# A layer norm's inverse deviation on GpSimd, a split group of attention matmuls, and fewer gather buffers in a two-layer metaformer kernel

## The chip, the cores and the metric

The kernel runs on one core of one Trainium2 chip. The metric is device time in microseconds (us) of one execution; the time given for a kernel is the median of its runs. The core has five engines that run their own instruction streams in order and meet at semaphores: PE (TensorE, matmuls), DVE (VectorE), ACT (ScalarE), POOL (GpSimd) and SP (SyncE, which here only issues DMAs). PEld is PE's weight load.

## What is computed

Input `x` is 8 images of 128 channels and 32 by 32 pixels, float32. Two layers follow each other; every one has a mixing step and a feed-forward step, each behind a normalisation and with a residual:

```python
x = x + attention(_ln_c(x))          # 8 heads, keys and queries over all 1024 pixels, softmax per row of 32 keys
t = t + stu(_ln_t(t))                # 16 spectral filters (causal convolutions) mixed by matrices, 4 resolutions
x = x + deformable_conv(_ln_c(x))    # 3 taps, each sample from 4 neighbouring pixels of a computed place
t = t + experts(_ln_t(t))            # 8 experts, the best 2 of a router
```

with

```python
def _ln_c(v, eps=1e-6):
    m = jnp.mean(v, axis=1, keepdims=True)
    s = jnp.var(v, axis=1, keepdims=True)
    return (v - m) / jnp.sqrt(s + eps)
```

In the attention `softmax` runs over the 32 keys of one image row (`axis=-1` of scores shaped batch, head, h, w, x, y), so that one query has 32 separate softmaxes, whose weighted values are added. The change touches the two normalisations that run inside the attention stage, the order of the attention's value matmuls, and the loads of the deformable convolution's samples.

## The kernel before

**Stages.** After a short start (about 30 us) comes the attention of all eight images, up to about 995 us. Then the spectral stage runs to about 2911 us: PE works through 4 groups of two images with 16 filters each (`filter_image`, L1355, and `mix`, L1343), and beside it, in slices that `advance` hands out, the second layer of the images of the group before (`DeformAndExperts.image`). The second layer of the last two images (`alone` is true) stands by itself at the end.

**The attention** (`attention_bounded`, L492 to L743) is written as a list of steps. `at(round, order, step)` puts a step into a round; the list is sorted by round, then by order, then by the place in the code, and emitted in that order under a manual schedule, so each engine's instruction order is what this list says. An image has 8 units (4 quarters of 256 queries times 2 groups of 4 heads), a unit has 4 rounds, so an image has 32 rounds and the stage 256. With `t0` the first round of a unit and `r` from 0 to 3:

- round `t0 + r`, order 0, `scores`: 8 matmuls on PE into `s`, a PSUM tile of which there is one (`bufs=1`); then one exponential on ACT, L606, 128 x 2048, into `e`, of which there are 11. The next round's scores overwrite `s`, so they wait for this exponential.
- round `t0 + r`, order 1, `add_tiles`: POOL adds the two halves of `e` into `t` (L615).
- round `t0 + 5`, order 4, `sums`: 16 matmuls into `z`; order 5, `reciprocals` on DVE (L629).
- round `t0 + 6`, order 2.5, `spread_out`: 4 matmuls that spread the reciprocals into `rb`.
- round `t0 + 6 + r`, order 3, `divide`: DVE multiplies `e` by `rb` (L643, 128 x 2048).
- round `t0 + 8 + r`, order 2, `values`: 8 matmuls of `e` into `av` (L653).

Order 6 is for the projections of the next image (`project_at`), the stores of results (`results`, one per two units, in round `t0 + 12` of the second) and the layer norm of the next image. I call the four rounds of a unit phases 0 to 3 (the round number modulo 4). Since units follow every four rounds, a phase 0 round holds scores, the first value group and a projection or a result's matmuls; phase 1 holds scores, the second value group and the 16 sums; phase 2 scores, the third group and the spreading; phase 3 scores, the fourth group and often a projection.

**The layer norm pieces** (`layer_norm_pieces`, L65) are 21 steps: 8 of statistics on DVE, then `guess` (4 instructions), three times `newton` (4 each) and `offset` (1), all on tiles of 128 x 8, and 8 of `norm` on ACT (L104), which need `offset`'s result `lp_nm`. `norm_at` gives their rounds, order 6: for images 2 to 7, counted from the first round of the image before, statistics in rounds 3 to 10, guess in 10, newton in 11, 11 and 12, offset in 12, and the eight `norm` in rounds 13 and 14, four in each. `FirstGroup.pieces` (L1187) uses the same steps for the first two images of the spectral stage, in the last image's rounds (order 7): the first image's statistics begin in round 8, its norms in round 20; the second's steps come 10 rounds later.

**The gathers** (`image`, L1030 to L1062): 24 points (8 token tiles, 3 taps), each an indirect DMA that POOL issues (L1043), 128 rows of 2 KB, into a buffer `g` of which there are 9; then 4 multiply-adds on DVE (L1058) per point. `fetch` is called 6 times ahead of the loop (3 times if `alone`), each followed by a `yield` unless `alone`, and once per point in it. `yield` hands control back to `advance`, so it moves where later steps stand in the instruction streams.

Of the kernel before, what the change touches and what calls it, by code (L numbers as in the profile page):

```python
# [11 lines left out]
F32 = mybir.dt.float32  # L12
I32 = mybir.dt.int32
AF = mybir.ActivationFunctionType
ALU = mybir.AluOpType
# [3 lines left out]
P = 128  # L19
B = 8  # L20
C = 128
T = 1024
NT = T // P
# [41 lines left out]
def layer_norm_pieces(nc, pool, src, dst, eps):  # L65

    t = {}

    def stats(i):
        if i == 0:
            for name, shape in (
                ("st", [P, NT, 6]), ("mv", [P, NT, 2]), ("v", [P, NT]), ("y", [P, NT]),
                ("w", [P, NT]), ("nm", [P, NT]),
            ):
                t[name] = pool.tile(shape, F32, tag=f"lp_{name}", name=f"lp_{name}")
            t["b"] = pool.tile([P, NT], I32, tag="lp_b", name="lp_b")
        nc.vector.bn_stats(t["st"][:, i, :], src()[:, i, :])
        nc.vector.bn_aggr(t["mv"][:, i, :], t["st"][:, i, :])  # L80

    def guess():
        v, y = t["v"], t["y"]
        nc.vector.tensor_scalar(v, t["mv"][:, :, 1], eps, None, ALU.add)
        nc.vector.tensor_scalar(t["b"], v.bitcast(I32), 1, None, ALU.logical_shift_right)
        nc.vector.tensor_scalar(
            y.bitcast(I32), t["b"], -1, 0x5F3759DF, ALU.mult, ALU.add
        )
        nc.vector.tensor_scalar(v, v, -0.5, None, ALU.mult)

    def newton():
        v, y, w = t["v"], t["y"], t["w"]
        nc.vector.tensor_mul(w, y, y)
        nc.vector.tensor_mul(w, w, v)
        nc.vector.tensor_scalar(w, w, 1.5, None, ALU.add)
        nc.vector.tensor_mul(y, y, w)

    def offset():
        nc.vector.scalar_tensor_tensor(
            t["nm"], t["mv"][:, :, 0], -1.0, t["y"], ALU.mult, ALU.mult  # L100
        )

    def norm(i):
        nc.scalar.activation(  # L104
            dst()[:, i, :], src()[:, i, :], AF.Identity, bias=t["nm"][:, i : i + 1],
            scale=t["y"][:, i : i + 1],
        )

    return (
        [partial(stats, i) for i in range(NT)] + [guess, newton, newton, newton, offset]  # L110
        + [partial(norm, i) for i in range(NT)]
    )
# [379 lines left out]
def attention_bounded(ctx, tc, ident, x, x1d, given, begin_group):  # L492
# [8 lines left out]
    nc = tc.nc  # L501
# [8 lines left out]
    sb = ctx.enter_context(tc.tile_pool(name="a_sb", bufs=2))  # L510
# [8 lines left out]
    for i in range(2):  # L519
        v = cp.tile([P, NT, VB], F32, name=f"vt{i}")  # L520
# [123 lines left out]
            e, e, un["rb"].unsqueeze(2).to_broadcast([P, NH, 2, QU]), ALU.mult  # L644
        )

    def values(img, un, r, qrt):
        hg = un["at"][1]
        if hg == 0 and r == 0:
            qrt["av"] = rp.tile([P, 512], F32, tag="av", name="av")  # L650
        for c in range(2):
            for j in range(NH):
                nc.tensor.matmul(  # L653
                    qrt["av"][32 * j : 32 * j + 32, 0:QU],
                    img["v"][:, 2 * r + c, P * hg + 32 * j : P * hg + 32 * j + 32],
                    un["e", r][:, j, c, :],
                    start=(hg == 0 and r == 0 and c == 0),
                    stop=(hg == HG - 1 and r == 3 and c == 1), skip_group_check=True,
                )
# [24 lines left out]
    def at(round_no, order, do, *args):  # L684
        work.append((round_no, order, len(work), do, args))

    def spread_rounds(pieces, rounds):
        for piece, round_no in zip(pieces, rounds):
            at(round_no, 6, piece)

    for b in range(B):
        img = {}
        first = 4 * UNITS * b
        project = [
            (keys, img, 0, 0), (keys, img, 0, 1), (queries, img, 0, 0),
            (keys, img, 1, 0), (keys, img, 1, 1), (queries, img, 1, 0),
            (key_values, b, img, 0), (key_values, b, img, 1),
            (queries, img, 0, 1), (queries, img, 1, 1),
        ]
        if b == 0:  # L700
            turn = {"tokens": (0, 0)}
            project_at = (-1, -1, -1, 1, 2, 3, 7, 8, 11, 12)
        else:
            project_at = [first + n for n in (-12, -9, -5, -4, -1, 3, 4, 7, 11, 12)]
            if b == 1:
                turn = {"load": 0, "tokens": (4, 6)}
                norm_at = (5,) * 4 + (7,) * 4 + (8, 8, 9, 9, 9) + (10,) * 4 + (11,) * 4
            else:
                turn = {"load": first - 36, "tokens": (first - 30, first - 26)}
                norm_at = [first - n for n in (  # L710
                    29, 28, 27, 26, 25, 24, 23, 22, 22, 21, 21, 20, 20, 19, 19, 19, 19, 18, 18, 18, 18
                )]
            turn["channels"] = (first - 17, first - 13)
        if b:
            at(turn["load"], 6, load, b)
            spread_rounds(
                layer_norm_pieces(nc, sb, lambda i=img: i["xt"], lambda: given.ht, 1e-6), norm_at
            )
            for par in range(2):
                at(turn["channels"][par], 5.5, channels, par)  # L720
        for par in range(2):
            at(turn["tokens"][par], 5.5, tokens, img, par)
        for step, when in zip(project, project_at):
            at(when, 6, *step)
        for qc in range(QC):
            qrt = {}
            for hg in range(HG):
                un = {"at": (qc, hg)}
                t0 = first + 4 * (HG * qc + hg)
                for r in range(4):  # L730
                    at(t0 + r, 0, scores, img, un, r)
                    at(t0 + r, 1, add_tiles, un, r)
                    at(t0 + 5, 4, sums, un, r)
                    at(t0 + 6 + r, 3, divide, un, r)
                    at(t0 + 8 + r, 2, values, img, un, r, qrt)
                at(t0 + 5, 5, reciprocals, un)
                at(t0 + 6, 2.5, spread_out, un)
            at(t0 + 11, 5, take, qrt)
            at(t0 + 12, 6, results, b, img, qc, qrt)
# [48 lines left out]
class DeformAndExperts:  # L788
# [182 lines left out]
    def image(self, b, x2, alone):  # L971
        nc, sb = self.nc, self.sb
# [46 lines left out]
        for tap in range(TAPS):  # L1019
            at = TAPS * C + 9 * tap  # L1020
# [9 lines left out]
        got = []  # L1030
        yield from self.corners(om, got)
        idx, w = got
# [6 lines left out]
        def fetch():  # L1039
            if len(fetched) < len(points):  # L1040
                i, tap = points[len(fetched)]
                g = sb.tile([P, 4 * C], F32, tag="g", name="g", bufs=9)
                nc.gpsimd.indirect_dma_start(  # L1043
                    out=g, out_offset=None, in_=rows,
                    in_offset=bass.IndirectOffsetOnAxis(ap=idx[:, i, tap : tap + 1], axis=0),
                )
                fetched.append(g)

        for _ in range(3 if alone else 6):
            fetch()  # L1050
            if not alone:
                yield
        yield
        yield
        for n, (i, tap) in enumerate(points):
            fetch()
            for k in range(4):
                nc.vector.scalar_tensor_tensor(  # L1058
                    x3[:, i, :], fetched[n][:, k * C : (k + 1) * C], w[:, i, tap, k : k + 1],
                    (tok if tap + k == 0 else x3)[:, i, :], ALU.mult, ALU.add,  # L1060
                )
            yield 1.7  # L1062
# [6 lines left out]
        got = []  # L1069
# [97 lines left out]
class FirstGroup:  # L1167
# [19 lines left out]
    def pieces(self, pool):  # L1187

        got = [(14, self.read), (3, partial(self.load, 0)), (4, partial(self.load, 1))]
        for n in range(2):  # L1190
            pieces = layer_norm_pieces(
                self.nc, pool, lambda n=n: self.ur[n], lambda n=n: self.ur[n], 1e-5
            )
            rounds = [*range(8, 21), *(20 + i // 2 for i in range(8))]
            got += [(r + 10 * n, piece) for r, piece in zip(rounds, pieces)]
        return got


# [258 lines left out]
def metaformer_kernel(  # L1457
# [25 lines left out]
    with tc.If(bounded > P - 1) as branch:  # L1483
        with ExitStack() as part:
            attention_bounded(part, tc, ident, x, x1d, given, begin.pieces)
# [66 lines left out]
```

## Time and profile before

| | us |
|---|---|
| runs of the kernel before | 3128.75, 3130.27, 3132.58 (median 3130.27) |
| the profiled execution's own time | 3137.39 |
| its span, from first to last instruction | 3135.6 |
| PE busy | 2793.4 (89%) |
| DVE, ACT, POOL busy | 1464.0 (47%), 978.7 (31%), 957.2 (31%) |

The durations below come from the profiled execution, 7 us above the median. "Busy" is the time in which an engine has an instruction in work, and the shares are averages over stages with different limits. A line of the timeline gives start, duration, engine, line, operation, output and inputs, count, and in brackets how long the engine had been idle and what ended that. A line of the groups gives the busy time of all, the mean of one in ns, and the idle time ahead of them.

### The profile page before, as it was taken

What the parts mean: (1) busy time and instruction counts of PE and PEld (TensorE: products, weight loads), DVE (VectorE), ACT (ScalarE), POOL (GpSimd) and SP (SyncE); (2) the same over time, 40 slices, a digit from 0 to 9 for tenths busy, and PEclk for the clock granted to TensorE, in tenths of its full rate; (3) what the DMA queues carried; (4) which work ended last, traced back from release to release, by engine and by line L of the source; (5) the groups of instructions that cost most, each with busy time, mean ns of one, the idle gap of its engine ahead of it and who ended that gap; (6) DMA issues with size and microseconds to landing.
All of it is one profiled execution on the core that took longest, in us unless ns stands there. A gap on an engine that the chain in (4) does not pass through costs nothing.

```text
span 3135.6 us, 45294 instructions
## 1 busy us (share of the span) xinstructions
PE 2793.4 (89%) x18896; PEld 1713.5 (55%) x18896; DVE 1464.0 (47%) x3035; ACT 978.7 (31%) x1198; POOL 957.2 (31%) x800
## 2 busy tenths in 40 slices
PE   7989889989986999999899899899899989899506
PEld 3545445545443666666566566566566656566202
DVE  4788788788786200000522440333522143332487
ACT  4666666666653111112112112212112211111100
POOL 4767667667663200000301300300300030300230
PEclk9999999999998999999999999999899999999758
DMA  0000000000001422210614411511611341610540
GB/s 25 2 15 15 1 15 15 2 15 9 2 28 40 115 61 65 76 48 27 201 41 124 124 34 41 171 58 58 184 34 48 107 121 34 191 51 14 175 146 14
DMA packets 177011, 199.80 MB, mean 64 GB/s; under 512 B 17236, under 2 KB 135188, under 8 KB 176800
## 3 DMA queue, kind: packets, MB, share of 16 engines
q1 hardware_dynamic: 147328, 134.97, 14.4%
q0 software_dynamic: 16800, 55.59, 5.8%
q10 hardware_dynamic: 12672, 6.29, 0.7%
q8 instruction: 150, 2.46, 0.3%
q14 instruction: 61, 0.50, 0.1%
HBM read 128.88 MB, written 67.92 MB: 63 GB/s over the span
## 4 chain that ended last, share of the span: by engine, by line
PE 54%; DVE 4%; another core or an unknown queue 3%; issue 1%; DMA 1%; ACT 1%; POOL 0%; ACTq 0%; POOLq 0%; DVEq 0%
PE pu L1355 33%; PE po L1343 15%; PE p_e L1076 3%; DVE x L1058 2%; PE p_g L1002 1%; DVE x L1082 1%; DMA tab<-gs 1%; PE p_out L1093 0%; PE p_out L1096 0%; PE p_turn L905 0%; PE p_l L1120 0%; DMA g<-tab,cn_idx 0%; ACT us L1359 0%; PE p_ut L1299 0%
## 5 line engine op out<-in xcount | busy, mean ns | idle before, releaser
L1359 ACT COPY us<-pu 128x512 f32<-128x512 f32 x512 | 300.1, 586 | 1382.0 <-PE pu L1355 1228.9
L615 POOL TENSOR_TENSOR t<-e 128x1024 f32<-128x1024 f32 x256 | 620.1, 2424 | 312.2 <-ACT e L606 312.2
L1355 PE MATMUL pu<-teto,ur 128*128 128x512 f32 (+3 forms) x2048 | 603.1, 438 | 51.3 <-ACT us L1359 40.1
L643 DVE TENSOR_TENSOR e<-e,rb 128x2048 f32<-128x2048 f32 x256 | 572.7, 2277 | 87.9 <-PE rb L636 85.6
L606 ACT ACTIVATE e<-s 128x2048 f32<-128x2048 f32 x256 | 480.9, 1878 | 293.2 <-PE s L601 291.6
L1355 PEld LDWEIGHTS pu<-teto,ur 128*128 128x128 f32 x2048 | 390.2, 192 | 330.7 <-issue 201.5
L1343 PE MATMUL po<-us,mf 128*128 128x128 f32 (+2 forms) x2048 | 530.8, 383 | 0.0
L601 PE MATMUL s<-q,k 32*128 32x256 f32 x4096 | 303.0, 411 | 37.0 <-ACT e L606 30.1
L1355 PE MATMUL pu<-teto,ht 128*128 128x512 f32 x992 | 292.2, 438 | 23.0 <-ACT us L1359 23.0
L653 PE MATMUL av<-e,vt 128*32 128x256 f32 x4096 | 283.2, 395 | 28.7 <-DVE e L643 23.8
L1043 POOL DMA_INDIRECT g<-tab,cn_idx x192 | 185.0, 964 | 377.2 <-DMA tab<-gs 194.3
L1355 PE MATMUL pu<-teto,xc 128*128 128x512 f32 x992 | 290.1, 435 | 2.9 <-issue 2.9
L1058 DVE SCALAR_TENSOR_TENSOR x<-g,w,x 128x128 f32<-128x128 f32 x704 | 250.3, 357 | 60.0 <-DVE x L1058 24.1
L601 PEld LDWEIGHTS s<-q,k 32*128 32x128 f32 x4096 | 190.2, 189 | 157.8 <-ACT e L606 101.2
L1355 PEld LDWEIGHTS pu<-teto,xc 128*128 128x128 f32 x992 | 188.7, 191 | 157.0 <-issue 116.9
L1343 PEld LDWEIGHTS po<-us,mf 128*128 128x128 f32 x2048 | 272.1, 193 | 4.1 <-issue 3.9
L757 POOL TENSOR_SCALAR rs_v<-rs_v 128x8 f32<-128x8 f32 x18 | 4.4, 246 | 875.2 <-DVE rs_b L755 875.2
L1082 DVE SCALAR_TENSOR_TENSOR x<-p_e,gates,x 128x128 f32<-128x128 f32 x512 | 177.6, 350 | 187.0 <-PE p_e L1076 170.8
L1355 PEld LDWEIGHTS pu<-teto,ht 128*128 128x128 f32 x992 | 189.6, 192 | 135.7 <-issue 67.0
L653 PEld LDWEIGHTS av<-e,vt 128*32 128x32 f32 x4096 | 108.9, 111 | 164.3 <-issue 72.7
L629 DVE RECIPROCAL r<-z 128x256 f32<-128x256 f32 x64 | 112.4, 1757 | 110.8 <-PE z L622 77.4
L1076 PE MATMUL p_e<-ew,tc 128*128 128x512 f32 x256 | 134.8, 633 | 14.0 <-DVE x L1082 8.9
(235 smaller groups left out, 1809.6 us busy)
## 6 DMA issues: line engine op xcount, KB each, us to landing
tab<-gs SPq DMA_DIRECT2D x168, 256.0 KB
mf<-mfd SPq DMA_DIRECT2D x48, 512.0 KB
teto<-in_phi_o SPq DMA_DIRECT2D x63, 256.5 KB
teto<-in_phi_e SPq DMA_DIRECT2D x63, 256.0 KB
mfd<-mf SPq DMA_DIRECT2D x16, 512.0 KB
tab<-gs ACTq DMA_DIRECT2D x24, 256.0 KB
xc<-in_x SPq DMA_DIRECT2D x8, 512.0 KB
x1d<-xt SPq DMA_DIRECT2D x8, 512.0 KB
```

The costliest lines, as they stand in the source:

```text
L601: nc.tensor.matmul(s[:, j, c, :], img["k"][rows, hg, 2 * r + c, :], q[rows, qc * QU : (qc + 1) * QU], start=True, stop=True,)
L606: nc.scalar.activation(e.rearrange("p j c q -> p (j c q)"), s.rearrange("p j c q -> p (j c q)"), AF.Exp, scale=float(HD) ** -0.5,)
L615: nc.gpsimd.tensor_add(t, e[:, :, 0, :], e[:, :, 1, :])
L643: nc.vector.tensor_tensor(e, e, un["rb"].unsqueeze(2).to_broadcast([P, NH, 2, QU]), ALU.mult)
L653: nc.tensor.matmul(qrt["av"][32 * j : 32 * j + 32, 0:QU], img["v"][:, 2 * r + c, P * hg + 32 * j : P * hg + 32 * j + 32], un["e", r][:, j, ...
L1043: nc.gpsimd.indirect_dma_start(out=g, out_offset=None, in_=rows, in_offset=bass.IndirectOffsetOnAxis(ap=idx[:, i, tap : tap + 1], axis=0),)
L1058: nc.vector.scalar_tensor_tensor(x3[:, i, :], fetched[n][:, k * C : (k + 1) * C], w[:, i, tap, k : k + 1], (tok if tap + k == 0 else x3)[: ...
L1076: nc.tensor.matmul(pe, tc[:, i * P : (i + 1) * P], self.ew[:, grp * 4 : grp * 4 + 4, :].rearrange("d e c -> d (e c)"), start=True, stop=True,)
L1082: nc.vector.scalar_tensor_tensor(x3[:, i, :], pe[:, k * C : (k + 1) * C], gate[:, i, grp * 4 + k : grp * 4 + k + 1], x3[:, i, :], ALU.mult ...
L1343: self.nc.tensor.matmul(out, lhsT, rhs, start=bank not in group["opened"], stop=last, skip_group_check=True)
L1355: nc.tensor.matmul(pu[:, i * P : HT], group["ur"][n][:, src * 4 + i, :], flt[:, 0 : HT - i * P], start=(i == 0), stop=(i == 3),)
L1359: nc.scalar.copy(us[:, n, :], pu)
```

## The change

The steps `guess`, `newton` and `offset` are issued on POOL in place of DVE. `guess` has three instructions in place of four (the shift by one bit and the product with -1 become one product with -0.5), `offset` two in place of one, so it is 17 instructions as before. Their rounds change for images 2 to 7: the statistics are in rounds 3, 3, 4, 4, 7, 7, 8, 8, guess in 8, newton in 9, 10 and 10, offset in 10, and the norms in rounds 11 to 14, two in each. For image 1 `norm_at` stays as it is. For the second image of the first group the steps come 4 rounds after the first image's in place of 10.

The second value group of each unit is split: the half for `c = 0` moves to the end of phase 0 (order 6.5), the half for `c = 1` stays in phase 1.

The gathers have 8 buffers in place of 9, and 3 calls of `fetch` stand ahead of the loop for all images, so images that are not `alone` have 3 calls and 3 `yield` fewer there.

```diff
@@ layer_norm_pieces
-            t["b"] = pool.tile([P, NT], I32, tag="lp_b", name="lp_b")
     def guess():
         v, y = t["v"], t["y"]
-        nc.vector.tensor_scalar(v, t["mv"][:, :, 1], eps, None, ALU.add)
-        nc.vector.tensor_scalar(t["b"], v.bitcast(I32), 1, None, ALU.logical_shift_right)
-        nc.vector.tensor_scalar(
-            y.bitcast(I32), t["b"], -1, 0x5F3759DF, ALU.mult, ALU.add
-        )
-        nc.vector.tensor_scalar(v, v, -0.5, None, ALU.mult)
+        nc.gpsimd.tensor_scalar(v, t["mv"][:, :, 1], eps, None, ALU.add)
+        nc.gpsimd.tensor_scalar(
+            y.bitcast(I32), v.bitcast(I32), -0.5, 0x5F3759DF, ALU.mult, ALU.add
+        )
+        nc.gpsimd.tensor_scalar(v, v, -0.5, None, ALU.mult)
 
     def newton():
         v, y, w = t["v"], t["y"], t["w"]
-        nc.vector.tensor_mul(w, y, y)
-        nc.vector.tensor_mul(w, w, v)
-        nc.vector.tensor_scalar(w, w, 1.5, None, ALU.add)
-        nc.vector.tensor_mul(y, y, w)
+        nc.gpsimd.tensor_mul(w, y, y)
+        nc.gpsimd.tensor_mul(w, w, v)
+        nc.gpsimd.tensor_scalar(w, w, 1.5, None, ALU.add)
+        nc.gpsimd.tensor_mul(y, y, w)
 
     def offset():
-        nc.vector.scalar_tensor_tensor(
-            t["nm"], t["mv"][:, :, 0], -1.0, t["y"], ALU.mult, ALU.mult
-        )
+        nc.gpsimd.tensor_mul(t["nm"], t["mv"][:, :, 0], t["y"])
+        nc.gpsimd.tensor_scalar(t["nm"], t["nm"], -1.0, None, ALU.mult)
@@ attention_bounded
-    def values(img, un, r, qrt):
+    def values(img, un, r, cs, qrt):
...
-        for c in range(2):
+        for c in cs:
...
                 norm_at = [first - n for n in (
-                    29, 28, 27, 26, 25, 24, 23, 22, 22, 21, 21, 20, 20, 19, 19, 19, 19, 18, 18, 18, 18
+                    29, 29, 28, 28, 25, 25, 24, 24, 24, 23, 22, 22, 22, 21, 21, 20, 20, 19, 19, 18, 18
                 )]
...
-                    at(t0 + 8 + r, 2, values, img, un, r, qrt)
+                at(t0 + 8, 2, values, img, un, 0, (0, 1), qrt)
+                at(t0 + 8, 6.5, values, img, un, 1, (0,), qrt)
+                at(t0 + 9, 2, values, img, un, 1, (1,), qrt)
+                at(t0 + 10, 2, values, img, un, 2, (0, 1), qrt)
+                at(t0 + 11, 2, values, img, un, 3, (0, 1), qrt)
@@ DeformAndExperts.image
-                g = sb.tile([P, 4 * C], F32, tag="g", name="g", bufs=9)
+                g = sb.tile([P, 4 * C], F32, tag="g", name="g", bufs=8)
...
-        for _ in range(3 if alone else 6):
+        for _ in range(3):
             fetch()
             if not alone:
                 yield
@@ FirstGroup.pieces
-            got += [(r + 10 * n, piece) for r, piece in zip(rounds, pieces)]
+            got += [(r + 4 * n, piece) for r, piece in zip(rounds, pieces)]
```

## The prediction

> **What bounds the kernel now.** I read the busy times by stretch first, to see which engine sets each stage, then one unit of the attention and one layer norm in the timeline, then the waits of PE in the spectral stage.
>
> ```profile
> core 0: us, PE busy (x) PEld busy (x) DVE busy (x) ACT busy (x) POOL busy (x), PEclk, DMA share, GB/s
> 50.00:300.00 250.00, 231.10 (x3012) 128.80 (x3000) 202.50 (x164) 156.42 (x132) 169.83 (x71) 0.97 0.02 8
> ...
> 1400.00:1700.00 300.00, 288.36 (x1174) 187.31 (x1173) 82.24 (x286) 61.88 (x111) 36.11 (x66) 0.98 0.28 83
> ...
> 2900.00:3136.00 236.00, 98.80 (x306) 50.04 (x304) 159.06 (x568) 20.74 (x42) 51.16 (x52) 0.69 0.37 111
> ```
>
> PE is fullest in the attention and the spectral stage, DVE at the end. In the attention no engine is full; a cycle of two engines sets the pace. PE's timeline of an ordinary phase 1, to the next scores:
>
> ```profile
> 502.25 1.15 PE L601 MATMUL s<-q,k 32*128 32x256 f32 x16 [0.39 <-ACT e L606]
> 503.32 1.07 PE L653 MATMUL av<-e,vt 128*32 128x256 f32 x16
> 504.21 1.91 PE L622 MATMUL z<-t,group 128*32 128x256 f32 x32
> 506.05 1.15 PE L601 MATMUL s<-q,k 32*128 32x256 f32 x16
> ```
>
> Scores, then the exponential (L606, 1.88), then the next scores: 1.15 + 1.88 and the hand-overs give 3.17 us, the shortest distance of two exponentials in the trace. A round takes longer where PE has more than 3.17 us of work: in phase 1 it is 1.07 (scores to values) + 1.0 (values) + 1.73 (sums) = 3.80. Over all 256 exponentials of ACT's timeline, images 1 to 6 take 115.5 to 118.2 us each; 32 rounds of 3.17 are 101.4. Of the 16 us between, 8 x 0.63 = 5 belong to phase 1, 1.9 to turning tokens, and about 9 to one place, the layer norm:
>
> ```profile
> 544.33 2.44 POOL L615 TENSOR_TENSOR t<-e 128x1024 f32<-128x1024 f32 x1 [0.45 <-ACT e L606]
> 544.34 2.45 DVE L96 TENSOR_TENSOR lp_y<-lp_y,lp_w 128x8 f32<-128x8 f32 x1
> ...
> 545.48 1.88 ACT L606 ACTIVATE e<-s 128x2048 f32<-128x2048 f32 x1 [0.58 <-PE s L601]
> ...
> 550.83 1.65 ACT L104 ACTIVATE ht<-xt,lp_nm,lp_y 128x128 f32<-128x128 f32 x4 [3.48 <-DVE lp_nm L99]
> ...
> 552.39 1.85 ACT L606 ACTIVATE e<-s 128x2048 f32<-128x2048 f32 x1
> ...
> 554.66 2.08 PE L636 MATMUL rb<-r,spread 64*128 64x256 f32 x8 [3.73 <-DVE r L629]
> ```
>
> Four norms stand ahead of an exponential on ACT and wait for DVE, which is late: a multiply of 8 columns took 2.45 us, just as long as POOL's addition beside it. The exponentials of rounds 13, 14, 15 then lie 6.9 and 6.6 apart here, and 9.6 and 6.5 in the other images. And PE, after 3.73 us without work, runs at half speed: these 8 matmuls take 2.08 us where an ordinary unit's take 1.14. Summed over images 1 to 6 the excess of rounds 13 to 15 over an ordinary round is 53.5 us (8.9 each); image 0 has 7.2 (rounds 10 and 11), the last image 13.4 (rounds 18 to 22 and 30).
>
> In the spectral stage PE is 96% busy, and its idle time has one name:
>
> ```profile
> PE pu L1355 <- ACT us L1359: 63.1, 5, 14.9
> ```
>
> The first such wait of ACT, in its timeline, has no releaser that the profile knows:
>
> ```profile
> 1541.15 0.59 ACT L1359 COPY us<-pu 128x512 f32<-128x512 f32 x1 [16.51 <-remote]
> ```
>
> In each of the six gather phases there, PE stands still for 10.6 to 14.9 us (74 us in all): some 10 us after the gathers' data begin to flow, ACT's copy starts 14 us after the matmul that it waits for, and goes on some 4 us after POOL first paused (at 1536.9, waiting for L1058). Until then POOL issued a gather every 1.25 us.
>
> **What the Trainium skill says.** SBUF — State Buffer, "SBUF: two separate sides": DVE and GpSimd share a port pair as an exclusive lock; a DVE operation with two SBUF inputs or in a two-port mode waits out the GpSimd operation. The trace agrees (2.45 us beside 2.44), and also that a DVE operation with one PSUM input isn't concerned: `divide` takes 2.28 us, and POOL's addition 2.43 beside it against 2.35 for the same size (L1033) in the spectral stage. TensorE: Matmul & The Clock Gate, "What's actually happening": a window of some 3.4 us of idleness halves the clock. Here gaps of 2.8 to 4.9 us were followed by half speed, for about 5.8 us; gaps of 1.5 us weren't.
>
> **The change, part by part.**
>
> *Values.* Half a group is 0.5 us. Phase 1 becomes 1.07 + 0.5 + 1.73 = 3.30. Phase 0 gains 0.5: in odd units it holds a projection (1.07 + 1.0 + 1.1 = 3.17, PE already full) and becomes 3.67, so the pair stays at 6.97; in even units it holds a result's matmuls (0.7), becomes 3.28, and the pair falls from 6.97 to 6.58. The half group needs `divide` of r = 1, which ends some 1.5 us into phase 0, so it doesn't wait. 4 pairs x 8 images + 2 (the last image has no projections late) = 34 x 0.39 = **-13**.
>
> *Norm on POOL.* DVE loses 17 small instructions per norm: 65 us over nine norms by the groups of lines L84 to L99. DVE isn't what bounds a unit; what counts is when `lp_nm` comes. POOL's small instructions in the spectral stage start 0.28 to 0.32 us apart (L757 to L762), so guess takes 0.9, newton 1.17, offset 0.6. For images 2 to 7, with round 9's scores as zero and rounds of 3.30, 3.17, 3.22: POOL does addition 8 to 2.5, then the addition of the results (L678, 2.35), which stands there too, to 4.8, guess to 5.7, addition 9 to 8.1, newton to 9.3, addition 10 to 11.7, two newtons and offset to 14.65. Round 12's scores start at 9.67, its exponential is due at 10.9. On ACT two norms stand ahead of it: they end at 15.45, so it ends at 17.35. PE has 3.67 of work in that round and then idles 4.0 us, so its clock falls: round 13 takes 6.1 in place of 3.3. Excess 4.06 + 2.8 = 6.9, against 8.9: 6 x 2.0 = **-12**. Later norms, two a round, take 0.8 us of ACT's 1.2 between exponentials. The sums of round 13 need addition 11, which ends as round 13 begins. The statistics, two in a round, fill DVE to within 0.2 us; I put that at nothing.
>
> Image 1's norm has no results' addition in its way, but 7 and 10 small instructions in two rounds: `lp_nm` 3.4 us into round 11, four norms, 3.9 + 2.7 = 6.6 against 7.2: **-0.5**. First group: newtons in three successive rounds make POOL late by 1.3 us; rounds 20 and 24 each wait 3.3 to 3.8 and then run at half speed: 12.8 against 13.4, **-0.6**; the norms leave the attention's tail, where the last sums came 2.4 us after the addition that they needed: **-2.4**.
>
> *Gathers.* In the built program POOL's 24 gathers of an image follow each other with nothing between, before and after. The number begun ahead only moves later steps; POOL's distance is set by the buffers. The three slots fewer cost nothing: PE needs the result 25 us after DVE has it (L905 after L780). With 8 buffers POOL waits for the use of the point 8 back: the first pause comes one gather, 1.3 us, earlier in each of the phases that I followed. If PE's stall ends that much earlier: 6 x 1.3 = **-8**. Bounds: -74, if all stalls go; +8, if the pauses only starve DVE. At the end, where DVE is the bound, a buffer less may cost up to 3.
>
> Sum: -13 - 12 - 0.5 - 0.6 - 2.4 - 8 = -36.5; 3137.4 becomes 3100.9, the median 3130.3 becomes **3094**.
>
> **The rivals.**
> - *The gather stalls mostly go.* They end after POOL pauses; earlier pauses might stop them from forming. Against: the start at 1.25 us a gather is the same, and the stall begins before any pause. Half of 74 in place of 8 gives 3065, all 3028.
> - *The norm moves nothing*, because POOL's chain is 2 us later than I reckon, and the gathers give nothing: only the values' 13 and the tail remain, 3115. For it: POOL is two thirds busy there, and each newton round already exceeds a 3.17 round.
> - *Slower: POOL's small instructions wait out `divide`.* If the lock worked that way, each of 14 instructions behind addition 9 could wait up to 2.28 us; all nine norms hold an exponential. At a mean wait of 0.55 us, 7.7 us per norm, +69 - 36: 3163. It decides from 4 us a norm, 0.29 us per instruction. Against: `divide` has a PSUM input, and POOL's addition lost only 0.08 us beside it.
> - That the gather edit doesn't do what it says, since POOL runs eight ahead, is part of my forecast.
>
> **How the numbers follow.** Forecast 0.62 (3076 to 3110 by itself); fewer stalls 0.16; norm moves nothing 0.13; slower 0.09. The range 3056 to 3119 leaves out the slower case and the larger half of the stalls' case, and takes in POOL 2 us late or early per norm. A measurement of this kernel tells 0.2% (6 us) from no change. Faster 0.88, same 0.04, slower 0.08.
>
> **What would show it.** Exponentials in phase 1 3.3 apart outside the norms; ACT waiting for POOL's `lp_nm` some 4.4 us ahead of each of nine first norms (40 in all, against 50.2 for DVE's now); half-speed matmuls in round 13; the six stalls still there, a little shorter; gathers still 1.25 us apart at first. Wrong, if small POOL instructions in the attention take over 0.5 us, or if PE's gaps at L1355 change by more than 20 us.

## The result, and the profile after

The changed kernel took 3094.94 us (median of 4 runs, 3088.86 to 3098.41), the kernel before 3131.43 in the same measurement (3128.75 to 3137.65): a ratio of 0.9879, with a 95% interval of 0.9857 to 0.9900. That is 36.5 us faster. The profiled execution of the changed kernel took 3088.86, its span is 3087.1; it is the fastest of its four, and the profiled one of before (3137.39) lies near the slowest of its own (3137.65), so the two spans lie 48.5 us apart, 12 more than the medians.

A stretch of the attention, in the columns of the prediction's first view:

```profile
50.00:300.00 250.00, 238.44 (x3100) 129.69 (x3092) 198.26 (x138) 160.02 (x135) 181.06 (x123) 0.99 0.04 12
```

In the attention PE gains (231.1 to 238.4 of 250 us), DVE sheds its small operations to POOL, and the granted clock is higher (0.97 to 0.99). PE's first spectral matmul moved from 996.6 to 957.5: **39.1 us, all that the medians show and more, come from the attention.** In the traces of two runs below that have the attention of before, PE's first spectral matmul stands at 991.8 and 995.1, so this difference is good to some 5 us.

I took the distances of successive exponentials in ACT's timeline; that of round 11 is the distance from its exponential to the next. The mean over images 1 to 6 (the images in whose rounds the norms of images 2 to 7 lie), in us, with three of the experiments below beside it (their rounds outside the table agree with those of the changed kernel to 0.02):

| round | before | after | late norms | POOL at the old rounds | DVE at the new rounds |
|---|---|---|---|---|---|
| even unit, phase 0 / 1 | 3.18 / 3.81 | 3.30 / 3.38 | 3.30 / 3.38 | 3.30 / 3.38 | 3.30 / 3.38 |
| odd unit, phase 0 / 1 | 3.18 / 3.81 | 3.71 / 3.37 | 3.71 / 3.37 | 3.71 / 3.37 | 3.71 / 3.37 |
| 10 | 3.17 | 3.16 | 3.16 | 3.16 | 12.94 |
| 11 | 3.17 | 7.17 | 3.17 | 3.17 | 4.10 |
| 12 | 3.19 | 4.10 | 3.71 | 3.71 | 3.58 |
| 13 | 9.16 | 4.15 | 3.74 | 5.84 | 3.39 |
| 14 | 6.51 | 3.20 | 3.24 | 3.35 | 3.26 |
| 15 | 3.39 | 3.17 | 3.17 | 3.56 | 3.17 |
| sum of 32 | 117.5 | 113.0 | 108.2 | 110.8 | 118.4 |

One norm in the changed kernel, in the timeline of POOL, DVE, ACT and PE (rounds 10 to 12 of an image; start, duration, then as before):

```profile
401.23 2.37 POOL L675 TENSOR_TENSOR xt<-xt,at 128x1024 f32<-128x1024 f32 x1
...
405.62 8.88 DVE L640 TENSOR_TENSOR e<-e,rb 128x2048 f32<-128x2048 f32 x4 [1.38 <-PE rb L633]
...
407.85 2.37 POOL L612 TENSOR_TENSOR t<-e 128x1024 f32<-128x1024 f32 x1
...
412.80 0.24 POOL L98 TENSOR_SCALAR lp_nm<-lp_nm 128x8 f32<-128x8 f32 x1
413.01 2.35 POOL L612 TENSOR_TENSOR t<-e 128x1024 f32<-128x1024 f32 x1
413.08 0.88 ACT L101 ACTIVATE ht<-xt,lp_nm,lp_y 128x128 f32<-128x128 f32 x2 [3.79 <-POOL lp_nm L98]
413.86 1.86 ACT L603 ACTIVATE e<-s 128x2048 f32<-128x2048 f32 x1
...
415.77 2.09 PE L598 MATMUL s<-q,k 32*128 32x256 f32 x16 [3.34 <-ACT e L603]
```

The chain is the one that the prediction drew: POOL adds the results (L675) and works off the additions late, `lp_nm` comes at 413.04, two norms and then the exponential follow on ACT, and PE's scores wait 3.34 us for that.

After this gap PE runs at half speed. The views by stretch show for how long (the third figure from the end is the granted clock, 1.00 for full speed). The first three lines are from a norm of the kernel before, behind the gap of 3.73 us in the prediction's lines, the others from the norm just shown:

```profile
554.05:557.46 3.41, 2.80 (x16) 1.90 (x20) 0.78 (x2) 1.73 (x5) 2.38 (x1) 0.50 0.00 0
557.46:560.88 3.42, 3.42 (x32) 1.43 (x27) 3.42 (x2) 1.92 (x2) 0.00 (x0) 0.50 0.03 7
560.88:564.29 3.41, 3.18 (x40) 1.89 (x38) 3.41 (x3) 2.52 (x3) 2.42 (x1) 1.00 0.00 0
...
411.98:415.39 3.41, 0.45 (x8) 0.00 (x0) 2.52 (x2) 2.31 (x3) 3.13 (x5) 1.00 0.00 0
415.39:418.80 3.41, 3.03 (x28) 1.77 (x32) 0.00 (x0) 2.42 (x5) 2.35 (x1) 0.50 0.00 0
418.80:422.20 3.40, 3.40 (x64) 1.88 (x60) 1.42 (x1) 2.15 (x4) 2.29 (x1) 1.00 0.00 0
```

At the norms of images 1 to 6 the half-speed stretches of the kernel before are 6.83 or 10.24 us long (51.2 us together), those of the changed kernel 3.41 us, one of them 6.83 (23.9 us together). The prediction read some 5.8 us for the kernel before from the lengths of the matmuls.

POOL's small operations take what they take in the spectral stage (203 and 235 ns there, L760 and L761 of the kernel before; 203 and 235 here, L92 and L93). In the groups of the changed kernel (busy time, mean ns of one, idle time ahead):

```profile
L93 POOL TENSOR_SCALAR lp_w<-lp_w 128x8 f32<-128x8 f32 x27 | 6.3, 235 | 2.4
```

None of them waits out `divide` (L640), which runs beside them, and the rival that made the kernel slower falls.

The waits of the changed kernel (engine, what waits, for what: us in total, times, longest):

```profile
PE pu L1356 <- ACT us L1360: 40.2, 4, 12.0
PE pu L1356 <- issue: 23.2, 6, 8.5
PE p_gt L1153 <- DVE gates L1149: 20.6, 7, 13.5
...
ACT ht L101 <- POOL lp_nm L98: 28.3, 8, 3.8
ACT xc L101 <- POOL lp_nm L98: 3.2, 1, 3.2
```

ACT waits 31.5 us in nine places for `lp_nm`. PE's six stalls at `pu` are there and shorter, 57 us by their gaps against 74. And one line is new: PE waits 7 times for DVE's `gates`, where the same view of the kernel before has 4 (17.1 us). The last two readings looked like a gain and a trifle; in the experiments the second is part of a loss, and the first couldn't be tried.

### The profile page after: what moved, and what is told of

It is laid out like the page before. It is cut to its first block, busy times and chain, and to the rows that moved or that the text cites. A ratio compares the mean times of both kernels' runs of the same rounds, so it can differ in the third digit from the quotient of the medians.

```text
span 3087.1 us, 45244 instructions
## 1 busy us (share of the span) xinstructions
PE 2792.3 (90%) x18896; PEld 1704.3 (55%) x18896; DVE 1401.7 (45%) x2882; ACT 977.1 (32%) x1198; POOL 976.0 (32%) x953
## 4 chain that ended last, share of the span: by engine, by line
PE 55%; DVE 5%; issue 2%; another core or an unknown queue 2%; DMA 1%; ACT 1%; POOL 0%; ACTq 0%; POOLq 0%; DVEq 0%
PE pu L1356 34%; PE po L1344 15%; PE p_e L1077 3%; DVE x L1059 2%; PE p_g L1003 1%; DVE x L1083 1%; DMA tab<-gs 1%; PE p_out L1094 1%; PE p_out L1097 1%; PE p_turn L906 0%; PE p_l L1121 0%; ACT us L1360 0%; PE p_ut L1300 0%; DMA g<-tab,cn_idx 0%
## 5 line engine op out<-in xcount | busy, mean ns | idle before, releaser
L612 POOL TENSOR_TENSOR t<-e 128x1024 f32<-128x1024 f32 x256 | 607.5, 2373 | 245.0 <-ACT e L603 245.0
L1356 PE MATMUL pu<-teto,ur 128*128 128x512 f32 (+3 forms) x2048 | 604.7, 439 | 40.4 <-ACT us L1360 29.1
L640 DVE TENSOR_TENSOR e<-e,rb 128x2048 f32<-128x2048 f32 x256 | 570.3, 2279 | 95.1 <-PE rb L633 93.7
L650 PE MATMUL av<-e,vt 128*32 128x256 f32 x4096 | 292.6, 393 | 6.1 <-DVE e L640 4.9
L650 PEld LDWEIGHTS av<-e,vt 128*32 128x32 f32 x4096 | 101.7, 110 | 150.3 <-issue 91.1
```

The source lines that it names most:

```text
L612: nc.gpsimd.tensor_add(t, e[:, :, 0, :], e[:, :, 1, :])
L640: nc.vector.tensor_tensor(e, e, un["rb"].unsqueeze(2).to_broadcast([P, NH, 2, QU]), ALU.mult)
L650: nc.tensor.matmul(qrt["av"][32 * j : 32 * j + 32, 0:QU], img["v"][:, 2 * r + c, P * hg + 32 * j : P * hg + 32 * j + 32], un["e", r][:, j, ...
L1356: nc.tensor.matmul(pu[:, i * P : HT], group["ur"][n][:, src * 4 + i, :], flt[:, 0 : HT - i * P], start=(i == 0), stop=(i == 3),)
```

## Experiments

These runs came from three chips (the results name them 1, 13 and 15; the chip of the first measurement isn't on record). There the kernel before takes 3038 to 3039 us in place of 3131, and PE has no stalls in the gather phases, as a wait of the kernel with 8 buffers and 6 ahead shows below. The attention's code is that of before in the kernel with 8 buffers, and the mean of images 1 to 6 is 117.5 us there as in the first profile, so what concerns the attention carries over; what the gathers' edit does to the stalls couldn't be tried. What a run gains on the kernel before, in us, is worked out from the ratio, which weighs all runs and isn't exactly the quotient of the medians: for the first four runs the medians differ by -13.4, -28.6, +5.5 and -0.7 us.

**The three edits, each alone.** Each is the kernel before with one part of the diff above: `values` and its steps; the norm with its rounds (and the 4 in place of 10); the gathers. The fourth has only the buffers:

```diff
-                g = sb.tile([P, 4 * C], F32, tag="g", name="g", bufs=9)
+                g = sb.tile([P, 4 * C], F32, tag="g", name="g", bufs=8)
...
         for _ in range(3 if alone else 6):
```

> Only the split of the values, the rest as before. My step said 34 pairs of units at 0.39 us: 13 us faster, ratio 0.9958. The rounds of the changed kernel's profile say otherwise: phase 1 went from 3.81 to 3.38, phase 0 from 3.17 to 3.30 in even units and to 3.71 in odd ones, which makes 0.21 us a pair: 7 us faster, ratio 0.9977. A third reading, that the split also brings the results of a unit earlier and helps the rounds of the norm, would show as more than 15 us.

Measured: 3025.91 against 3039.29 us, ratio 0.9965 (0.9952 to 0.9977), 10.6 us faster. The interval takes in both 7 and 13. The rounds outside the norm decide: phase 1 gains 0.43, phase 0 loses 0.12 in even units and 0.53 in odd ones, 0.21 us a pair, the smaller of the two readings.

> Only the layer norm (POOL in place of DVE, new rounds, second image 4 rounds behind), the rest as before. My step said 12 + 0.5 + 0.6 + 2.4 = 15.5 us faster, ratio 0.995. The rounds of the changed kernel's profile give the norm what the values leave of the attention's 39 us: 32 us, ratio 0.990. If the two edits need each other (the norm's wait is shorter only because the values left phase 1), the norm alone gives well under 25 and the sum of both alone stays behind 39.

Measured: 3010.66 us, 0.9915 (0.9901 to 0.9929), 25.8 us faster. That is above my 15.5 and below the 32 left over; the norm's gain doesn't hang on the values.

> Only the gathers (8 buffers, 3 begun ahead), the rest as before. My step: six stalls of PE shorter by 1.3 us, 8 us faster at the most, less up to 3 us at the end: ratio 0.9975 to 0.9985. By the two profiles the spectral stage is 11.5 us shorter and the end 2 us longer: 0.997. Rival: this difference is that of two executions, and the edit gives nothing: 1.000.

Measured: 3044.75 us, 1.0022 (1.0014 to 1.0031). The edit alone costs 6.7 us here (5.5 by the medians), which no theory had said.

> 8 buffers but still 6 gathers begun ahead of the loop. If the number begun ahead is without effect, because POOL issues all 24 in a row whatever it is, the same ratio as with 3 ahead, within 0.001. If the number ahead is what counts, 1.000 here and a gain there.

Measured: 3038.56 us, 1.0003 (0.9995 to 1.0011). So to do without the ninth buffer costs nothing here; what costs is the three calls of `fetch`, with their `yield`, that are missing ahead of the loop, which I had put at zero. PE's waits tell where. With 8 buffers and 6 ahead:

```profile
PE p_gt L1152 <- DVE gates L1148: 17.0, 4, 13.5
...
PE pu L1355 <- issue: 2.4, 1, 2.4
```

and with 8 buffers and 3 ahead:

```profile
PE p_gt L1152 <- DVE gates L1148: 20.6, 7, 13.5
...
PE p_back L1109 <- ACT ot L1099: 0.7, 3, 0.2
```

`pu` has one short wait, so there is no stall on this chip. Three `yield` fewer move every later step of the second layer three slots ahead in PE's stream, the transpose `p_gt` of the router's gates among them. In the first image of each group it now stands ahead of DVE's result: 3 waits more, 1.18 us each, and `p_back` adds 0.7, together 4.3 us of PE's idle time. By PE's first and last spectral matmul that stage is 1816.0 us long with 3 ahead, 1811.2 with 6; in the two such pairs of traces further below it is 5.6 and 5.9 us longer with 3 ahead, and what follows it 2 to 3 us shorter in all three. So the waits explain most of the stage's loss, but the stages together lose 2 to 4 us, less than the medians of the first two pairs say (5.5 and 6.1); the rest is open. No run calls `fetch` three times ahead and keeps the six `yield`, so that the slots do it, and not the number of gathers begun, is argued from these waits.

**The whole and its parts together.** The changed kernel again, and the same with the gathers of before:

> The changed kernel itself, beside the same runs of the kernel before as the next three. If the three edits add up, the product of the three alone: 0.9965 x 0.9915 x 1.0022 = 0.990. If the gathers' edit gains only where PE stalls in the gather phases, and it does not stall here, this is above the first measurement's 0.9879; with stalls in the runs of before it is near it.

Measured: 3003.10 against 3038.36 us, 0.9887 (0.9871 to 0.9904), in agreement with the first measurement, though no stall is there to be shortened. The interval takes in both 0.9879 and the product 0.990, so it doesn't decide between the two expectations.

> Values and norm together, the gathers as before (9 buffers, 6 ahead). If gathers with 8 buffers and 3 ahead cost 7 us where PE has no stalls, this is 7 us faster than the changed kernel beside it: 0.988 if that has 0.990. If the two edits of the attention overlap in the rounds 12 to 14, 0.989 to 0.990.

Measured: 2997.05 us, 0.9867 (0.9851 to 0.9883): without the gathers' edit the kernel is 6 us faster (its slowest run took 2998.63, the fastest with the edit 3001.10). Values and norm together give 40.4 us, alone 10.6 and 25.8 (13.4 and 28.6 by the medians), so no interaction of the two can be told.

**The engine or the rounds?** The norm's edit moves the steps to POOL and to earlier rounds. One run keeps only the rounds, one only the engine:

```diff
     def guess():
         v, y = t["v"], t["y"]
-        nc.gpsimd.tensor_scalar(v, t["mv"][:, :, 1], eps, None, ALU.add)
+        nc.vector.tensor_scalar(v, t["mv"][:, :, 1], eps, None, ALU.add)
...
```

> The changed kernel, with guess, newton and offset on DVE again, at the new rounds. My theory: DVE's small operations with two SBUF inputs each wait out a POOL addition (2.4 us), so lp_nm comes about as late behind its guess as before, round 11 takes 9 us and round 12 6.5, and the norm's gain is lost: 20 to 27 us slower than the changed kernel, ratio to before 0.996 to 1.000. Rival: the new rounds and two norms a round bring the gain, whatever the engine: within 6 us of the changed kernel.

Measured: 3039.47 us, 1.0005 (0.9997 to 1.0014): 36 us slower than the changed kernel beside it, more than expected, and by another way than `lp_nm`. The timeline of one such norm:

```profile
533.43 2.29 DVE L85 TENSOR_SCALAR lp_b<-lp_v 128x8 int32<-128x8 int32 x1
535.75 4.64 DVE L86 TENSOR_SCALAR lp_y<-lp_b 128x8 int32<-128x8 int32 x1
...
540.38 2.27 DVE L643 TENSOR_TENSOR e<-e,rb 128x2048 f32<-128x2048 f32 x1
542.58 1.75 DVE L629 RECIPROCAL r<-z 128x256 f32<-128x256 f32 x1
...
533.33 2.37 POOL L678 TENSOR_TENSOR xt<-xt,at 128x1024 f32<-128x1024 f32 x1
535.65 4.72 POOL L615 TENSOR_TENSOR t<-e 128x1024 f32<-128x1024 f32 x2
...
544.38 2.08 PE L636 MATMUL rb<-r,spread 64*128 64x256 f32 x8 [7.90 <-DVE lp_w L93]
```

The two operations of 8 columns end when POOL's additions beside them end (L85 at 535.72 with L678 at 535.70, L86 at 540.39 with the pair of L615 at 540.37). Here POOL's work is back to back, so two operations of `guess` hold DVE for 7 us; the `divide` and the reciprocals queued behind it are late, and PE stands still for 7.90 us (the wait is put down to DVE's next operation, L93; what PE needs is the reciprocals' `r`). This is what the Trainium skill says in SBUF — State Buffer, "SBUF: two separate sides" (whichever starts first holds the shared pair for its whole instruction and the other blocks), now for an operation with one SBUF input too; the same section counts two-port modes among those concerned, and no trace tells whether these operations ran in one. That POOL's second addition comes first again, ahead of an operation that already waits (its 4.64 us span both additions), is what this trace adds.

```diff
                 norm_at = [first - n for n in (
-                    29, 29, 28, 28, 25, 25, 24, 24, 24, 23, 22, 22, 22, 21, 21, 20, 20, 19, 19, 18, 18
+                    29, 28, 27, 26, 25, 24, 23, 22, 22, 21, 21, 20, 20, 19, 19, 19, 19, 18, 18, 18, 18
                 )]
```

> The changed kernel, POOL for guess, newton and offset, but at the old rounds for images 2 to 7 (guess 10, newton 11, 11, 12, offset 12, norms 13 and 14, four each). If POOL makes lp_nm come late only through what stands ahead of it there (in the new rounds the results' addition of 2.4 us in round 8), the wait in round 13 is some 2.7 us in place of 3.5 and four norms instead of two follow it: excess per image 3.5 to 5 against 5.2, so from equal to 9 us faster than the changed kernel, 0.9855 to 0.9885. If the new rounds were needed, slower than 0.991.

Measured: 2993.35 against 3037.99 us, 0.9853 (0.9838 to 0.9868), about 10 us faster than the changed kernel's 0.9887 (another chip, each beside its own runs of before). POOL at the rounds of before is the better half of the edit; the new rounds take some of it back. In its timeline:

```profile
413.73 0.24 POOL L98 TENSOR_SCALAR lp_nm<-lp_nm 128x8 f32<-128x8 f32 x1
...
414.00 1.65 ACT L101 ACTIVATE ht<-xt,lp_nm,lp_y 128x128 f32<-128x128 f32 x4 [2.38 <-POOL lp_nm L98]
...
417.46 1.15 PE L598 MATMUL s<-q,k 32*128 32x256 f32 x16 [2.38 <-ACT e L603]
418.54 1.74 PE L650 MATMUL av<-e,vt 128*32 128x256 f32 x16
```

Two rounds later, the results' addition no longer stands between the last statistics and `lp_nm`: ACT waits 2.38 us and PE's gap is 2.38. The scores after it run at full speed (1.15 for 16; 2.09 in the changed kernel), but the values behind them don't (1.74 in place of 1.07): this gap too is followed by a half-speed stretch of 3.41 us. So it is in three of the images 1 to 6; in the other three, with gaps of 2.38 to 2.42 us, none follows. One of each, by stretch:

```profile
415.39:418.80 3.41, 1.34 (x24) 0.90 (x27) 3.41 (x2) 3.41 (x6) 2.21 (x2) 1.00 0.03 5
418.80:422.21 3.41, 3.41 (x28) 1.97 (x24) 3.41 (x3) 2.75 (x4) 2.49 (x2) 0.50 0.00 0
...
524.62:528.03 3.41, 1.65 (x20) 0.79 (x12) 1.98 (x2) 2.80 (x5) 2.76 (x3) 1.00 0.00 0
528.03:531.44 3.41, 2.73 (x36) 1.56 (x36) 3.41 (x3) 3.41 (x6) 2.38 (x1) 1.00 0.03 5
```

**No wait at all.** If that wait is all that is left, norms that stand later on ACT cost nothing. `channels` needs the first four norms by round 15, the others by round 19:

```diff
-                norm_at = (5,) * 4 + (7,) * 4 + (8, 8, 9, 9, 9) + (10,) * 4 + (11,) * 4
+                norm_at = (5,) * 4 + (7,) * 4 + (8, 8, 9, 9, 9, 13, 13, 14, 14, 15, 16, 17, 18)
...
-                    29, 29, 28, 28, 25, 25, 24, 24, 24, 23, 22, 22, 22, 21, 21, 20, 20, 19, 19, 18, 18
+                    29, 29, 28, 28, 25, 25, 24, 24, 24, 23, 22, 22, 22, 19, 19, 18, 18, 17, 16, 15, 14
...
-            rounds = [*range(8, 21), *(20 + i // 2 for i in range(8))]
+            rounds = [*range(8, 21), *(22 + i // 2 for i in range(8))]
```

> The changed kernel, with the norms two rounds later: rounds 13, 13, 14, 14, 15, 16, 17, 18 for images 1 to 7 and two rounds later for the first group. If ACT's wait for POOL's lp_nm is all that is left of the norm's cost, rounds 11 to 13 fall from 7.17, 4.10 and 4.15 to 3.17, 3.71 and 3.37 in six images (31 us), image 1's from 14.5 to 10 (4), the last image's waits go (6): 41 us faster than the changed kernel, 0.977 of before. If POOL is then late for the sums of round 13, some 4 us of each image come back: 15 to 20 us faster only.

Measured: 2962.29 us, 0.9748 (0.9732 to 0.9764): 40.8 us faster than the changed kernel beside it, as expected; by PE's first spectral matmul (956.2 and 917.4) 38.9 us of it lie in the attention. Between 50 and 900 us the granted clock is 1.00 (0.98 in the changed kernel). Its timeline has norms between exponentials, with no wait for POOL:

```profile
402.58 0.86 ACT L101 ACTIVATE ht<-xt,lp_nm,lp_y 128x128 f32<-128x128 f32 x2
404.53 1.88 ACT L603 ACTIVATE e<-s 128x2048 f32<-128x2048 f32 x1 [1.09 <-issue]
406.30 0.87 ACT L101 ACTIVATE ht<-xt,lp_nm,lp_y 128x128 f32<-128x128 f32 x2
407.74 1.88 ACT L603 ACTIVATE e<-s 128x2048 f32<-128x2048 f32 x1 [0.58 <-ACT ht L101]
```

Round 13 stays 0.37 above an ordinary phase 1 (3.74 against 3.37); so little of the second theory is there.

**Two smaller steps on top.** The late norms with the gathers of before, and then with the split in even units alone:

```diff
+                if hg == 0:
+                    at(t0 + 8, 6.5, values, img, un, 1, (0,), qrt)
+                    at(t0 + 9, 2, values, img, un, 1, (1,), qrt)
+                else:
+                    at(t0 + 9, 2, values, img, un, 1, (0, 1), qrt)
```

> The changed kernel with the late norms, and the gathers as in the kernel before (9 buffers, 6 ahead). With 3 ahead, PE's p_gt stands ahead of DVE's gates in three images more (1.18 us each) and p_back in three (0.24 each). If that is what the gathers cost, this is 4 to 6 us faster than the late norms alone (0.9748): 0.973. If PE has slack there once the attention is shorter: 0.9748.

Measured: 2960.22 us, 0.9744 (0.9731 to 0.9757). `p_gt` waits 3 times less and the spectral stage is 5.9 us shorter (1812.1 against 1818.0), but what follows it is 1.9 longer (230.0 against 228.1), and the ratios can't be told apart. A gain of up to 5 us isn't excluded, and isn't shown.

> As the run before it, and the values split in even units alone. In odd units the half group makes phase 0 0.53 us longer (a projection stands there) and phase 1 only 0.43 shorter. If the phases add, 0.1 us in each of some 28 odd units: 3 us faster than the run before it. Rival: the longer phase 0 also covers the norm's and DVE's lateness: no difference, or slower.

Measured: 2958.54 us, 0.9744 (0.9730 to 0.9757). An odd unit's phases do gain 0.1 us (phase 0 3.17, phase 1 3.80), but round 13 rises from 3.74 to 4.27 and the last image loses 0.8; no difference can be measured. The best versions are these and the late norms, 41 to 45 us faster than the changed kernel's 3003 (2.5% under the kernel before).

## Why the prediction came out

The predicted 3094 was met within 1 us, and the chain that it drew for the norm is the one in the trace, but every large term of the sum was off and they cancelled out: that the total fits so well is luck. Term by term, with what the two profiles and the experiments show:

| term | predicted | measured |
|---|---|---|
| values | -13 | -8 by the rounds (-7.0 to -14.6 alone) |
| norm, images 2 to 7 | -12 | -22.5 |
| norm, image 1; first group; tail | -0.5; -0.6; -2.4 | -2.7; -4.6; -1.6 |
| gathers | -8 | +6 without stalls; with stalls open |
| sum | -36.5 | -36.5 (medians; the lines without the gathers make -39.4) |

- *Values.* Phase 0 came out as reckoned (3.67 predicted and 3.71, 3.28 and 3.30), phase 1 not: 3.38 in place of 3.30. The forecast had 1.0 for the value group and 1.73 for the sums; its own lines have 0.89 from the values to the sums (503.32 to 504.21) and 1.84 from there to the next scores (504.21 to 506.05). The whole, 3.80, was right, but half a group then saves 0.44 and not 0.5, and 0.43 was measured. So small an error halves the gain of a pair: 0.21 in place of 0.39. The odd units lose 0.1.
- *Norm: the wait.* "they end at 15.45 ... Excess 4.06": measured, round 11 is 4.00 above 3.17. ACT waits 3.5 us on the mean (31.5 over nine) where 4.4 was said. "DVE isn't what bounds a unit; what counts is when `lp_nm` comes" isn't borne out. In the kernel before PE waits in the norm's rounds for DVE's reciprocals (the 3.73 us of the prediction's lines), and with DVE at the new rounds it stands still for 7.90 us for them: POOL also gains by freeing DVE's queue.
- *Norm: the clock.* "PE ... then idles 4.0 us, so its clock falls: round 13 takes 6.1 in place of 3.3": this step failed. PE idles 3.34 us, and rounds 12 and 13 together lose 4.10 + 4.15 - 3.71 - 3.37 = 1.17 us in place of 2.8, so the excess is 5.2, not 6.9, and the gain 8.9 - 5.2 = 3.75 an image. I had carried the loss of the kernel before over to another gap: there two or three steps of 3.41 us run at half speed, here mostly one. In the repeated run of the changed kernel the same gap (3.31) left the scores at full speed and slowed the sums behind them (3.17 for 32 matmuls, 1.91 ordinarily). The Trainium skill (TensorE: Matmul & The Clock Gate, "What's actually happening") says that PE's activity is judged in a window of some 3.4 us that runs freely, whatever the kernel does. The traces agree: half speed comes in steps of 3.41 us on a fixed grid (the last section), so where the loss falls depends on where in the grid the gap lies.
- *First group and image 1.* The same too large clock term: the last image's excess is 8.8 in place of 12.8, image 1's 4.5 in place of 6.6. The tail came out nearly as said.
- *Gathers.* "The number begun ahead only moves later steps ... The three slots fewer cost nothing: PE needs the result 25 us after DVE has it" failed: I had checked one hand-over (L905) and not every PE instruction among the steps that move. `p_gt` is a later one, with no such slack. And "If PE's stall ends that much earlier: 6 x 1.3 = -8": the first two profiles show stalls shorter by 17 us in all, but the two executions lie near opposite ends of the two kernels' spreads. The attention gained 39.1 and the medians 36.5, so no gain of the rest can be told from the 5 us by which the attention itself varies.
- *Rivals.* The slower one is refuted (200 to 240 ns an operation). "The norm moves nothing" is refuted by the norm alone (-25.8). That the stalls mostly go isn't what the first profile shows (57 us of 74 are left).

What stays open: why PE stalls in the gather phases in the first measurement and not in the runs on three chips, where POOL issues the gathers at the same 1.25 us. The stalls make up most of the 92 us between the two times of the kernel before.

## What to carry to other kernels

When a small chain feeds an in-order engine that sets the pace, look first at where its consumer stands in that engine's queue: here two to four rounds of delay for the eight norms were worth 41 us, more than all three edits together, and nothing needed to become faster. That holds where the chain holds up nothing else: on DVE it delayed the reciprocals, and late norms with the chain on DVE weren't run. When a step is moved by slots, list every instruction that moves with it and the slack of each, not that of the best known one. A total that comes out right says nothing on its terms; run the edits one at a time.

## What the runs showed of the hardware

- In the attention of the 13 traces, the half-speed stretches of an execution start whole numbers of 3.41 us apart (to 0.01 us) and are 3.41 us or a multiple long. I cut the attention, from 45 us on, into steps on that grid. Of 3324 steps at full speed, all 90 in which PE was busy for less than 41.1% were followed by half speed, none of the 3225 with 44.5% or more, and six of the nine between. After a half-speed step another one followed in all 56 cases with PE busy for less than 85%, in none of the 78 above 91%, and in three of the 14 between.
- So the size of a gap alone doesn't tell what it costs. A gap of 2.38 us left 1.34 of 3.41 us busy (39%) and was followed by half speed; one of 2.42 us, cut in two by the grid, left 1.65 (48%) and wasn't. Of the 18 gaps of 3.31 to 3.43 us in three traces (the changed kernel, its repetition, and it with the gathers of before), 16 were followed by one step and two by two.
- A single-input DVE operation on 128 x 8 elements took 4.64 us while POOL ran two additions back to back: it can wait out more than one POOL instruction. In the kernel before, the same operation (L86) took 1.40 us on the mean of nine.
- The kernel before took 3131 us in one measurement and 3038 to 3039 in the others. In the profile of the kernel with 8 buffers and 6 ahead (3037.27), which takes as long as the kernel before in its measurement, the attention is like that of the first measurement's profile (117.5 us an image); the spectral stage took 1906.9 us in the first measurement against 1811.2, 77 us of the difference in PE's idle time.
